# Half-array products of a pair side by side, PSUM in two rotations, and whole products for the last six batches

## The chip, the cores and the metric

The kernel runs on one core of a Trainium2 chip. A core has TensorE (PE, matrix products into PSUM), VectorE (DVE), ScalarE (ACT), GpSimd (POOL) and SyncE (SP, which here issues DMAs). The metric is the device time of one execution in microseconds (us). It was 3108.3 us as the median of three runs (3107.53 to 3109.01).

## The reference

The input x has 128 batches of 128 nodes with 512 features, in fp32; adj is 128x128. Four layers follow each other, each of them `x = layernorm(x + layer(x))`:

```python
# layer 0, W1 = W2 = adj, so that C - A is the bias b alone
A = einsum('od,bdn->bon', W1, x);  C = einsum('od,bdn->bon', W2, x) + b[None, :, None]
out = max(relu(A[:, :, None, :] + (C - A)[:, :, :, None]), axis=-1)
# layer 1: attention with 8 heads of 64 over the 128 nodes
q, k, v = (x @ Wq + bq), (x @ Wk + bk), (x @ Wv + bv)      # each reshaped to (b, n, 8, 64)
scores = einsum('bqhd,bkhd->bhqk', q, k) / sqrt(64) + (1 - adj) * -1e9
out = einsum('bhqk,bkhd->bqhd', softmax(scores), v).reshape(b, n, 512) @ Wo + bo
# layer 2: graph attention
h = x @ W;  e = leaky_relu(h @ a1 [:, :, None] + h @ a2 [:, None, :], 0.2) * adj
out = elu(softmax(e, axis=2) @ h + beta * h)
# layer 3: graph convolution
out = (D^-1/2 adj D^-1/2) @ (x @ weight) + bias
```

## The kernel before

**The planner.** The kernel's work is cut into some 13,000 steps: a name and a batch number, for example ("SC", 60). `STEPS` gives each step its engine, a cost, what it comes after, and the buffers that it takes with the steps that free them. `list_order` is a list scheduler that runs while the kernel is built: it takes the step that can start first by those costs, and among TensorE's steps the one with the lowest `rank`, which is the batch number plus a constant of the step from the table `LAG` minus one from `LEAD`. The instructions are issued in that fixed order. On the chip each engine works through its own queue in order, and waits at an instruction until what it depends on is done. `POOLS` is the number of buffers of each kind; the planner's idea of time has no effect on the chip beyond the order that it leaves.

**The steps of a batch.** Even and odd batches form pairs. LD loads x; A, R and AP0 are layer 0 with its norm. MX1 and MX2 write x to DRAM and read it back turned, TX transposes it in blocks of 32 on VectorE, so that xT is there for the products. RL reads x back for the residual (x2), C1 adds the bias row. The attention: Q, K, V are products with the weights; SC makes the scores of all heads; M adds the mask on VectorE and moves the scores to SBUF; SM1, EXP, SMR, SMN are the softmax (row maximum, exponential, reciprocal, scaling); MS1 and MS2 take the probabilities through DRAM, TS transposes them on VectorE in blocks of 32; O multiplies them with v, and OE copies the result. Y is the product with Wo, then Y1, Q1, P1, AP1 the norm (statistics, `rstd` and `off` on ScalarE, the power -1/2 on POOL, application on ScalarE). Layer 2: L (two dot products), E, EZ, E1, EE, E2 (the softmax), BT and BE (its transpose), GT and GE, U (the product), U1, UE, U2, UP (elu and residual), norm U3 to AP2. Layer 3: NX, NE, C3, Z (the product), norm Z1 to AP3, OUT. The norms' scalars are made once for a pair.

**The products.** `seven` computes a 512x512 product for a pair by seven half-size products instead of eight (P1 to P7), from sums S1 to S4 that POOL makes of the left operand and from weight differences T1 to T4 that are made once; T1 is written over the upper right quarter of the weights, W[0,1]. The seven products run in three PSUM accumulators (px: P1, P2; py: P6, P7, P4; pz: P5, P3), which ScalarE (`u`, `C11`) and VectorE (`U2`, `U3`, `C11`, `C21`, `C22`, `C12`) read out between them; R1 and R2 on POOL add `u` to the residual. Q and K form their result turned, as eight matmuls with 128 columns for a product, the others as four with 256.

**Half-array products.** A score has a contraction over 64 features only, so SC's matmuls use 64 rows of the array each, and two heads (`par` 0 and 1) run in the two halves of the rows. O's results have 64 rows for a head, so its matmuls use 64 columns each. Both are sixteen matmuls for a batch, as the profile counts them: it shows every fp32 matmul of the program as two records, and counts of matmuls in this document are those of the records. In the planner such steps have a `mode`, "row" or "col"; entering or leaving modes costs 0.1 (`SWITCH`), and steps with a mode are drawn together by `CLOSE`. In the order that results, a batch's SC and some other batch's O stand next to each other 107 times, and each of them stands alone 21 times.

**PSUM.** Its eight banks are: one for px, two for py, one for pz, two ("tr") shared by everything else, and two ("sc") for the scores of one batch, one for each `par`.

Lines that matter below: L693 the products of `seven`, L669 its sums on POOL, L752 and L745 its additions on VectorE, L875 the matmuls of SC, L891 M, L906 and L920 the exponential and the scaling, L932 MS2, L940 TS, L950 O, L960 the copies OE, GE, NE, L997 E, L1004 to L1015 EZ and E1, L1035 BT, L1095 NX, L625 the application of a norm.

Of the kernel before, what the change touches and what calls it, by code (L numbers as in the profile page):

```python
# [24 lines left out]
SWITCH = 0.1  # L25
CLOSE = 2.0
REST, WAKE = 1.4, 3.7


class Step:  # L30
# [12 lines left out]
    def __init__(self, engine, cost, *after, takes=(), soon=0.0, batches=None, port=False, mode="",  # L43
                 dma=(), rush=0.0):
        self.port = port or engine == "POOL"
        self.mode, self.dma, self.rush = mode, dma, rush
        self.engine, self.cost, self.after = engine, cost, after
        self.takes, self.soon = dict(takes), soon
        self.batches = batches or (lambda b: True)

    def buffers(self, b):

        return {p: r for p, r in self.takes.items() if b % 2 == 0 or p not in PAIRS}

    def others(self, name, b):
        if name.endswith("+"):
            return [(name[:-1], b), (name[:-1], b ^ 1)]
        if name.endswith("-1"):
            return [(name[:-2], b - 1)]
        if name.endswith("-2"):  # L60
            return [(name[:-2], b - 2)]
        if name.endswith("@"):
            return [(name[:-1], b) for b in (0, 1)]
        return [(name, b)]


def list_order(steps, rank, pools, n):
# [14 lines left out]
    while todo:  # L82
        best = None
        for k in can:
            s = steps[k[0]]
            t = max(ready[k], free.get(s.engine, 0.0), free.get("port", 0.0) if s.port else 0.0)
            for p in s.buffers(k[1]):
                if len(taken[p]) >= pools[p]:
                    for r in taken[p][-pools[p]]:
                        t = max(t, ends.get(r, 1e9) + SIGNAL)  # L90
            if t >= 1e9:
                continue
            if s.engine == "PE":
                key = (t, rank(*k) - (CLOSE if mode and s.mode else 0.0), k)
            else:
                key = (t, ready[k] - s.soon - (s.rush if k[1] < 4 else 0.0), k)
            if best is None or key < best:
                best = key
        t, _, k = best
# [3 lines left out]
        if s.engine == "PE":  # L103
# [4 lines left out]
            if bool(s.mode) != bool(mode):  # L108
                cost += SWITCH
# [8 lines left out]
        for p, readers in s.buffers(k[1]).items():  # L118
# [28 lines left out]
def late(b):  # L147
    return b >= 4


POOLS = {
    "px": 1, "py": 2, "pz": 1, "tr": 2, "sc": 1, "x": 4, "xB": 2, "xT": 2,
    "qT": 2, "kT": 1, "v": 2, "s": 1,
    "sB": 1, "sT": 1, "oT": 1, "x2": 3, "z": 1, "e": 2, "bT": 2, "gT": 1, "m": 1, "x3": 2,
# [7 lines left out]
    "ROW": Step("PE", 3.5, "BV", "BO", takes={"tr": ("ROW1",)}, batches=first),  # L162
    "ROW1": Step("DVE", 0.7, "ROW", batches=first),
    "LOG": Step("DVE", 5.7, "BETA", "A1", batches=first, port=True),
    "LOG1a": Step("PE", 0.45, "LOG", takes={"tr": ("LOG2a",)}, batches=first),
    "LOG1b": Step("PE", 0.45, "LOG", takes={"tr": ("LOG2b",)}, batches=first),
# [3 lines left out]
    "NORM1": Step("PE", 0.2, "NORM", takes={"tr": ("NORM2",)}, batches=first),  # L170
# [3 lines left out]
    "ADJ": Step("PE", 0.2, ("LD", 2.3), takes={"tr": ("ADJ1",)}, batches=first),  # L174
    "ADJ1": Step("DVE", 0.3, "ADJ", batches=first),
    "A": Step("PE", 0.87, "LD", "A-1", "ADJ1@", takes={"tr": ("R",)}),
# [7 lines left out]
    "PT": Step("PE", 0.5, "PX", takes={"tr": ("PTE",)}, batches=early),  # L184
# [5 lines left out]
    "SC": Step("PE", 1.09, mode="row", takes={"sc": ("M",)}),  # L190
    "M": Step("DVE", 1.33, "SC", "MASK@", takes={"s": ("MS1",)}),
# [5 lines left out]
    "MS2": Step("SP", 1.9, "MS1", takes={"sB": ("TS",)}, dma=(4.2, 1.4)),  # L197
    "TS": Step("DVE", 1.18, "MS2", takes={"sT": ("O",)}),
    "O": Step("PE", 1.02, "TS", "VE", "O-1", takes={"tr": ("OE",), "oT": ("Y+",)}, mode="col"),
    "OE": Step("ACT", 0.5, "O"),  # L200
    "Y1": Step("DVE", 0.82, takes={"t1": ("AP1+",)}, soon=20),
    "Q1": Step("ACT", 0.4, "Y1+", soon=20, batches=even),
    "P1": Step("POOL", 0.58, "Q1", soon=20, batches=even),
    "AP1": Step("ACT", 1.03, "P1+", soon=20),
    "L": Step("DVE", 1.45, "AP1", "LOG2a@", "LOG2b@", soon=20, port=True),
    "E": Step("PE", 0.12, "L", takes={"tr": ("E1",)}),
# [4 lines left out]
    "BT": Step("PE", 0.12, "E2", takes={"tr": ("BE",), "bT": ("GT",)}),  # L211
    "BE": Step("ACT", 0.2, "BT", soon=20),
    "GT": Step("PE", 0.89, "BE", "GT-1", takes={"tr": ("GE",), "gT": ("U+",)}),
# [5 lines left out]
    "Q2": Step("ACT", 0.4, "U3+", soon=20, batches=even),  # L219
    "P2": Step("POOL", 0.58, "Q2", soon=20, batches=even),  # L220
    "AP2": Step("ACT", 1.03, "P2+", soon=20),
    "NX": Step("PE", 0.89, "AP2", "NX-1", "NORM2@", takes={"tr": ("NE",), "nx": ("Z+",)}),
# [3 lines left out]
    "Q3": Step("ACT", 0.4, "Z1+", batches=even),  # L226
    "P3": Step("POOL", 0.58, "Q3", batches=even),
    "AP3": Step("ACT", 1.03, "P3+"),
# [16 lines left out]
def sum_steps(n, engine_needs, readers):  # L245

    for i in range(4):
        needs = engine_needs if i == 0 else [f"{n}S{i}"]
        takes = {"SX" if n == "X" else "S": readers} if i == 0 else {}
        STEPS[f"{n}S{i+1}"] = Step("POOL", 0.75, *needs, takes=takes, batches=even, rush=30)  # L250


def seven_steps(n, sums, needs, weights, pool, out, add=(), turned=False, copy=False, T="POOL"):
# [5 lines left out]
    def step(name, engine, cost, *after, takes=(), soon=0.0):  # L259
        after = [(sums if a[0] == "S" else n) + a if isinstance(a, str) else a[0] for a in after]  # L260
        STEPS[n + name] = Step(engine, cost, *after, takes=takes, soon=soon, batches=even)
# [7 lines left out]
    parts += [f"{sums}S{i}" for i in (1, 2, 3, 4)]  # L269
    for s in STEPS.values():  # L270
# [7 lines left out]
        "px": (n + "C11",), "u": (last,), **({"uL": (n + "C21",)} if turned else {}), **out  # L278
    })
    step("P6", "PE", c, "S2", "P1", (n + "T2@",), takes={"py": (n + "C21",)})  # L280
    step("P5", "PE", c, "S1", "P6", takes={"pz": (n + "C12",)})
# [28 lines left out]
for n, needs, letters in (  # L310
# [12 lines left out]
}  # L323
STEPS["SC"].after = ("SC-1", *done["Q"], *done["K"])
STEPS["O"].after = ("TS", "O-1", *done["V"])
STEPS["Y1"].after = tuple(done["Y"])
STEPS["U1"] = Step("ACT", 0.55, *done["U"], takes={"m": ("U2",)}, soon=20)
STEPS["Z1"].after = tuple(done["Z"])
# [3 lines left out]
    "A": 0.325, "QP2": 15.731, "QP7": 15.871, "QP1": 16.057, "QP6": 16.294, "KP6": 16.456,  # L332
    "VP6": 16.608, "QP4": 16.618, "KP1": 17.099, "KP2": 17.121, "KP7": 17.182,
    "KP4": 17.445, "QP5": 17.471, "QP3": 17.625, "KP5": 17.893, "SC": 17.957, "KP3": 18.214,
    "VP1": 18.457, "VP3": 18.722, "VP2": 18.760, "VP4": 18.799, "VP7": 18.889,
    "VP5": 19.214, "O": 21.214, "UP6": 21.481, "YP6": 21.817, "YP1": 22.204, "YP7": 22.289,
    "YP5": 22.388, "YP2": 22.535, "YP3": 22.760, "YP4": 22.812, "UP1": 23.048, "E": 23.322,
    "BT": 23.666, "UP4": 23.847, "GT": 24.012, "UP3": 24.212, "UP7": 24.308, "UP5": 24.501,
    "UP2": 24.787, "NX": 26.260, "ZP3": 26.496, "ZP6": 27.211, "ZP2": 27.845, "ZP1": 27.849,
    "ZP7": 28.155, "ZP4": 28.327, "ZP5": 28.337,  # L340
# [3 lines left out]
    "BT57": 0.32, "O57": 0.32, "Z57": 0.26, "A58": -0.04, "GT58": 0.17, "O58": 0.23, "V58": -0.04,  # L344
    "V59": -1.28, "NX60": 1.25, "Z60": -0.11, "BT61": -0.13, "GT61": 1.45, "O61": 0.43,
    "Y61": -0.05, "Z61": 0.32, "BT62": 0.05, "NX62": 2.93, "U62": -1.85, "Y62": 0.33,
    "BT63": -0.05, "GT63": -0.43, "NX63": 0.07, "O63": 0.21, "U63": 0.77, "V63": -0.28,
}


def rank(name, b):
    if name not in LAG:
        return -1.0
    stage = name[0] if name[1:2] == "P" else name
# [4 lines left out]
def kernel(  # L359
# [39 lines left out]
    def mm_tile(name):  # L399
        return psum.tile([P, 512], F32, tag="tr", name=name, bufs=2)  # L400

    def tr_tile(name):
        return psum.tile([P, C, P], F32, tag="tr", name=name, bufs=2)
# [182 lines left out]
    pa, po, pg, pn, do = {}, {}, {}, {}, {}  # L586
# [12 lines left out]

    def ready(layer, b, shift=None):  # L600

        mv = mean_var.pop((layer, b // 2))
        for held, name in ((rstd, "rstd"), (off, "off")):
            pair_tiny(held, name, layer, b, 1)
        r, o = rstd[layer, b // 2][:, :, 0], off[layer, b // 2][:, :, 0]
# [12 lines left out]
    def power(layer, b):  # L618
        r = rstd[layer, b // 2][:, :, 0]
        nc.gpsimd.tensor_tensor(r, r, neg_half.to_broadcast([P, 2]), ALU.pow)  # L620
# [14 lines left out]
    def seven(n, w, operand, sums, tag, result, added=None, bias=None, scale=1.0):  # L635
# [36 lines left out]
        def P_(name, bank, left, right, new=False):  # L672
            def step(b):
                if new:
                    pool = ("px", "py", "pz")[bank]
                    ps[b, bank] = psum.tile(
                        [P, quarter], F32, tag=pool, name=f"{pool}_{n}{b}", bufs=POOLS[pool]
                    )
# [88 lines left out]
        C_("C12", 2, 0, hi, "own")  # L767
        for i in range(4):
            do[f"{n}T{i}"] = T(i)
# [95 lines left out]
    def SC(b):  # L865
# [3 lines left out]
            psum.tile([P, H // 2, P], F32, tag="sc", name=f"ps_s_{b}_{par}")  # L869
# [17 lines left out]

    def M(b):
        s = probs[b] = buf("s", [P, Q, H, S], b)
        for par, ps in enumerate(scores.pop(b)):  # L890
            nc.vector.tensor_tensor(  # L891
                by_head(s)[:, par * C : (par + 1) * C],
                ps.rearrange("p h (q s) -> p h q s", s=S),
                mask.rearrange("p (q s) -> p q s", s=S)[:, None].to_broadcast([P, C, Q, S]),
                ALU.add,
            )
# [41 lines left out]
    def TS(b):  # L938
        sT[b] = buf("sT", [P, H, P], b)
        nc.vector.transpose(  # L940
            sT[b].rearrange("p h (q s) -> p q h s", s=S), dp.pop(b)
        )

    def O(b):
        ps = tr_tile(f"ps_o_{b}")
        t, vb = sT.pop(b), v.pop(b)[:, b % 2]
        for c in range(C):
            for par in range(2):
# [4 lines left out]
                    rhs=t[:, par * C + c, :],  # L953
# [11 lines left out]
    with_sums("Y", seven("Y", wo_sb, lambda b: oT[b], {}, "x2", x2, x2))  # L965
# [94 lines left out]
    with_sums("U", seven("U", w2_sb, lambda b: gT[b], {}, "x3", x3))  # L1060


    def U1(b):
        m[b] = buf("m", [P, D], b)
        nc.scalar.activation(m[b], x3[b][:, b % 2], AF.Relu, scale=-1.0)
# [4 lines left out]
    def U2(b):  # L1070
        u = x3[b][:, b % 2]
# [119 lines left out]
```

## Time and profile before

| | |
|---|---|
| median of three runs | 3108.3 us |
| the profiled execution, its time | 3107.76 us |
| its span (first to last instruction) | 3106.0 us |
| TensorE busy | 3058.3 us, 98% |
| VectorE / ScalarE / POOL busy | 2346.7 / 2216.0 / 1700.1 us |
| granted TensorE clock, mean | 0.993 |
| SC: matmuls, busy | 2048, 149.2 us |
| O: matmuls, busy | 2048, 140.1 us |

The profiled execution is 1.76 us longer than its span, which is the time around the first and the last instruction. A group's line has, in order: line, engine, operation, output and inputs by the program's names, shapes, count, then busy time and the mean duration of one instruction, and after the second bar the idle time of that engine just before them with what ended it. Matmuls overlap in the records, so durations add up to more than the time they take; the distance between starts is what a step costs TensorE. The granted clock is the share of the full TensorE clock that the throttle allowed in a stretch.

### The profile page before, as it was taken

The numbers are of one execution on the slowest core, as the hardware profiler recorded it, in microseconds if no ns is written. First come the engines' busy times: TensorE is split into PE (matmuls) and PEld (weight loads), VectorE is DVE, ScalarE is ACT, GpSimd is POOL, SyncE is SP. The second block draws the span as 40 slices with busy tenths as digits, with TensorE's granted clock in tenths as the row PEclk, the third lists the DMA queues.
The fourth block names the chain that finished last, engine by engine and source line by source line (L and its number), as shares of the span: only waits on it lengthen the run. The fifth ranks groups of instructions, "written<-read, shape, count | busy, mean of one in ns | idle before, by whom it ended". The sixth has DMA issues, their size and how long they took to land.

```text
span 3106.0 us, 61445 instructions
## 1 busy us (share of the span) xinstructions
PE 3058.3 (98%) x21026; PEld 2709.3 (87%) x21026; DVE 2346.7 (76%) x5418; ACT 2216.0 (71%) x7234; POOL 1700.1 (55%) x1946
## 2 busy tenths in 40 slices
PE   7999999999999999999999999999999999999996
PEld 5888888888888888888888888888888889889875
DVE  6877777777777777777777777777777777777674
ACT  4787777777777777777777777777777777766664
POOL 4345555555655655555555556556555555556475
PEclk8999999999999999999999999999999999999998
DMA  7533332323323323323323233233233232222210
GB/s 211 163 108 102 105 103 96 109 91 108 103 96 102 110 96 103 100 96 105 103 96 109 91 107 103 96 103 109 96 103 100 97 104 89 86 79 89 74 57 28
DMA packets 234457, 312.38 MB, mean 101 GB/s; under 512 B 27680, under 2 KB 156832, under 8 KB 234144
## 3 DMA queue, kind: packets, MB, share of 16 engines
q1 hardware_dynamic: 232368, 307.40, 30.2%
q8 instruction: 166, 2.72, 0.4%
q10 hardware_dynamic: 1776, 1.05, 0.2%
q14 instruction: 147, 1.20, 0.1%
HBM read 174.14 MB, written 134.22 MB: 99 GB/s over the span
## 4 chain that ended last, share of the span: by engine, by line
PE 95%; DVE 1%; DMA 1%; POOL 1%; ACT 1%; issue 1%; ACTq 0%; POOLq 0%; SPq 0%; DVEq 0%
PE py_Q L693 6%; PE py_V L693 6%; PE py_K L693 5%; PE py_U L693 5%; PE py_Y L693 5%; PE py_Z L693 5%; PE ps_s L875 4%; PE ps_o L950 4%; PE px_Y L693 4%; PE px_K L693 4%; PE ps_nx L1095 4%; PE pz_K L693 4%; PE px_Q L693 4%; PE px_U L693 4%; PE ps_gT L1048 4%; PE pz_Q L693 4%
## 5 line engine op out<-in xcount | busy, mean ns | idle before, releaser
L620 POOL TENSOR_TENSOR rstd<-rstd,neg_half 128x2 f32<-128x2 f32 x256 | 176.8, 698 | 508.6 <-ACT rstd L606 505.4
L625 ACT ACTIVATE x<-x,off,rstd 128x512 f32<-128x512 f32 x512 | 417.0, 814 | 17.1
L906 ACT ACTIVATE s<-s,mx 128x128 f32<-128x128 f32 x1024 | 395.6, 391 | 18.9 <-DVE mx L900 15.1
L597 DVE BATCH_NORM_STATS2 st<-x 128x6 f32<-128x512 f32 x512 | 346.7, 677 | 10.3 <-POOL x L1076 5.5
L920 ACT ACTIVATE s<-s,sm 128x128 f32<-128x128 f32 x1024 | 313.5, 393 | 6.5 <-DVE sm L915 5.7
L1076 POOL TENSOR_TENSOR x<-x,x 128x512 f32<-128x512 f32 x128 | 162.8, 1272 | 183.1 <-DVE x L1072 174.7
L984 DVE SCALAR_TENSOR_TENSOR junk<-x,wa_bc 128x512 bf16<-128x512 f32 x256 | 230.0, 898 | 16.4 <-ACT x L625 5.5
L669 POOL TENSOR_TENSOR S_U<-gT 128x256 f32<-128x256 f32 x128 | 117.2, 915 | 189.9 <-ACT gT L960 189.7
L606 ACT ACTIVATE rstd<-mv,eps_c 128x2 f32<-128x2 f32 x256 | 75.6, 295 | 200.6 <-DVE mv L598 194.0
L826 POOL TENSOR_TENSOR x<-x,bo_bc 128x512 f32<-128x512 f32 x128 | 160.7, 1277 | 98.2 <-DMA x<-dx 88.2
L1109 POOL TENSOR_TENSOR x<-x,b_bc 128x512 f32<-128x512 f32 x128 | 162.8, 1272 | 64.5 <-PE ps_nx L1095 57.7
L906 ACT ACTIVATION_READ_ACCUMULATOR s<-s,mx 128x1 f32 x1024 | 194.7, 190 | 0.0
L940 DVE STREAM_TRANSPOSE sT<-sB 128x1024 f32<-128x1024 f32 x128 | 158.8, 1240 | 35.7 <-PE ps_o L950 35.5
L891 DVE TENSOR_TENSOR s<-ps_s,mask 128x512 f32<-128x512 f32 x256 | 162.2, 674 | 10.1 <-PE ps_s L875 5.7
L624 ACT ACTIVATE off<-off,rstd 128x1 f32<-128x1 f32 x512 | 147.2, 288 | 21.5 <-POOL rstd L620 21.4
L1040 ACT COPY bT<-ps_bT 128x128 f32<-128x128 f32 x128 | 33.9, 265 | 175.9 <-PE ps_bT L1035 175.6
L1095 PEld LDWEIGHTS ps_nx<-naT,x 128*128 128x128 f32 x1024 | 131.6, 195 | 29.3 <-issue 23.0
L900 DVE TENSOR_REDUCE mx<-s 128x8 f32<-128x1024 f32 x128 | 153.9, 1203 | 0.2
L875 PEld LDWEIGHTS ps_s<-kT,qT 64*128 64x128 f32 x2048 | 124.5, 187 | 33.4 <-issue 30.7
L875 PE MATMUL ps_s<-kT,qT 64*128 64x128 f32 x2048 | 149.2, 285 | 0.4 <-DVE s L891 0.3
L752 DVE TENSOR_TENSOR x<-py_Z,x 128x256 f32<-128x256 f32 x192 | 80.4, 419 | 90.0 <-PE py_Z L693 87.1
L669 POOL TENSOR_TENSOR S_Y<-oT 128x256 f32<-128x256 f32 x128 | 93.5, 731 | 95.1 <-ACT oT L960 73.5
(180 smaller groups left out, 9312.7 us busy)
## 6 DMA issues: line engine op xcount, KB each, us to landing
dp<-s SPq DMA_DIRECT2D x128, 512.0 KB, 2.6
sB<-dp SPq DMA_DIRECT2D x512, 128.0 KB, 2.8
x<-in_x SPq DMA_DIRECT2D x128, 256.0 KB, 3.2
dx<-x SPq DMA_DIRECT2D x128, 256.0 KB, 4.4
x<-dx SPq DMA_DIRECT2D x64, 512.0 KB, 4.0
out_x<-x SPq DMA_DIRECT2D x128, 256.0 KB, 2.0
xB<-dx SPq DMA_DIRECT2D x496, 64.0 KB, 2.0
wk_sb<-in_L_gnn_Wk SPq DMA_DIRECT2D x4, 256.0 KB, 8.3
```

What stands on the lines that cost most here:

```text
L597: nc.vector.bn_stats(st, t)
L620: nc.gpsimd.tensor_tensor(r, r, neg_half.to_broadcast([P, 2]), ALU.pow)
L625: nc.scalar.activation(dst, src, AF.Identity, bias=shift, scale=scale)
L669: nc.gpsimd.tensor_tensor(s[:, i], x, y, op)
L693: nc.tensor.matmul(to, lhsT=one, rhs=two, start=(new and k == 0), stop=(k == 1), skip_group_check=True,)
L875: nc.tensor.matmul(scores[b][par][:, c, :], lhsT=qT[b][rows, c, cols], rhs=kT[b][rows, c, cols], start=True, stop=True,)
L906: nc.scalar.activation(s[:, :, h], s[:, :, h], AF.Exp, bias=mx[:, h : h + 1], accum_out=sums[b][:, h : h + 1],)
L920: nc.scalar.activation(s[:, :, h], s[:, :, h], AF.Identity, scale=sm[:, h : h + 1])
L984: nc.vector.scalar_tensor_tensor(junk, x2[b][:, b % 2], 1.0, wa_bc[i], op0=ALU.mult, op1=ALU.mult, accum_out=s12[b][:, i : i + 1],)
L1076: nc.gpsimd.tensor_tensor(t, t, x2.pop(b)[:, b % 2], ALU.add)
L1095: nc.tensor.matmul(ps[:, c, :], lhsT=x3[b][:, b % 2, c * P : (c + 1) * P], rhs=naT, start=True, stop=True,)
L1109: nc.gpsimd.tensor_tensor(t, t, b3_bc, ALU.add)
```

## The change

It has four parts.

1. *Order.* The planner's costs of entering a mode are set apart (`ENTER`: row, col and back to whole-array products), steps of the same mode are drawn together more strongly, a mode step may be chosen up to 0.15 ahead of its being ready (`AWAIT`), and SC and O of both batches of a pair get the same batch number in `rank`. `LAG` and `LEAD` have new values throughout. In the order that results there are 59 groups of SC, O, O, SC in direct succession (the scores of one pair and the outputs of an earlier pair), 3 of SC and O, 2 of O and O, 7 lone SC and 3 lone O.
2. *PSUM.* The banks px, py, pz and tr become one rotation of five (`ps`), and the scores a rotation of three (`sc`). M becomes M0 and M, one for each half of the heads, so that the first bank is free after M0.
3. *Transposed probabilities.* TS writes over its input: `sB` has two buffers, `sT` is gone. O's moving operand is then four runs of 32 elements instead of one run of 128, and `sB` is freed by O instead of by TS.
4. *The last six batches* (from `LAST` = 122 on) form Y, U and Z as whole products, batch by batch: F0 and F1 of 8 matmuls each, into one bank, added to the residual by YFE and ZFE (U's product is read by U1 and U2 directly). The overwritten quarter of the weights is read again from DRAM by YR, UR and ZR on SP's queue, after the last seven of that product. The norms Q1 to Q3 and P1 to P3 run for single batches there.

```diff
-SWITCH = 0.1
+ENTER = {"row": 0.2, "col": 0.15, "": 0.205}
 CLOSE = 2.0
+AWAIT = 0.15
...
-            if s.engine == "PE":
-                key = (t, rank(*k) - (CLOSE if mode and s.mode else 0.0), k)
+            if s.engine != "PE":
+                key = (t, ready[k] - s.soon - (s.rush if k[1] < 4 else 0.0), k, t)
+            elif mode and s.mode:
+                near = CLOSE + (CLOSE if s.mode == mode else 0.0)
+                key = (max(t - AWAIT, free["PE"]), rank(*k) - near, k, t)
             else:
-                key = (t, ready[k] - s.soon - (s.rush if k[1] < 4 else 0.0), k)
+                key = (t, rank(*k), k, t)
...
 POOLS = {
-    "px": 1, "py": 2, "pz": 1, "tr": 2, "sc": 1, "x": 4, "xB": 2, "xT": 2,
+    "ps": 5, "sc": 3, "x": 4, "xB": 2, "xT": 2,
     "qT": 2, "kT": 1, "v": 2, "s": 1,
-    "sB": 1, "sT": 1, "oT": 1, "x2": 3, "z": 1, "e": 2, "bT": 2, "gT": 1, "m": 1, "x3": 2,
+    "sB": 2, "oT": 1, "x2": 3, "z": 1, "e": 2, "bT": 2, "gT": 1, "m": 1, "x3": 2,
...
-    "SC": Step("PE", 1.09, mode="row", takes={"sc": ("M",)}),
-    "M": Step("DVE", 1.33, "SC", "MASK@", takes={"s": ("MS1",)}),
+    "SC": Step("PE", 0.895, mode="row", takes={"sc": ("M0",), "sc+": ("M",)}),
+    "M0": Step("DVE", 0.665, "SC", "MASK@", takes={"s": ("MS1",)}, soon=3),
+    "M": Step("DVE", 0.665, "M0", soon=3),
...
-    "MS2": Step("SP", 1.9, "MS1", takes={"sB": ("TS",)}, dma=(4.2, 1.4)),
-    "TS": Step("DVE", 1.18, "MS2", takes={"sT": ("O",)}),
-    "O": Step("PE", 1.02, "TS", "VE", "O-1", takes={"tr": ("OE",), "oT": ("Y+",)}, mode="col"),
+    "MS2": Step("SP", 1.9, "MS1", takes={"sB": ("O",)}, dma=(4.2, 1.4)),
+    "TS": Step("DVE", 1.18, "MS2"),
+    "O": Step("PE", 0.875, "TS", "VE", "O-1", takes={"ps": ("OE",), "oT": ("Y+",)}, mode="col"),
...
-    "Q1": Step("ACT", 0.4, "Y1+", soon=20, batches=even),
+    "Q1": Step("ACT", 0.4, "Y1", "Y1*", soon=20, batches=normed),
...
+    STEPS[n + "R"] = Step("SP", 0.4, n + "P5-2", dma=(2.5, 0.9), batches=lambda b: b == LAST)
+    STEPS[n + "F0"] = Step("PE", 1.74, need, n + "R%", n + "F0-1", takes={"ps": (end,), **out}, batches=last)
+    STEPS[n + "F1"] = Step("PE", 1.74, n + "F0", batches=last)
+STEPS["YFE"] = Step("DVE", 0.69, "YF1", "C1", soon=20, batches=last)
+STEPS["ZFE"] = Step("DVE", 0.69, "ZF1", "C3", soon=20, batches=last)
...
+    if name in ("SC", "O") and b in BOTH:
+        b |= 1
     return b + LAG[name] - LEAD.get(f"{stage}{b // 2}", 0.0)
...
+        def again(b):
+            nc.sync.dma_start(
+                out=T1, in_=source[:quarter, hi].rearrange("(c p) f -> p c f", p=P)
+            )
+        def whole(half):
+            def step(b):
+                if half == 0:
+                    ps[b] = mm_tile(f"p_{n}{b}")
+                cols = (lo, hi)[half]
+                for k in range(C):
+                    nc.tensor.matmul(
+                        ps[b][:, cols],
+                        lhsT=operand(b)[:, b % 2, k],
+                        rhs=w[:, k, cols],
+                        start=(half == 0 and k == 0),
+                        stop=(k == C - 1),
+                        skip_group_check=True,
+                    )
+                if half == 1:
+                    full[b] = ps.pop(b)
+            return step
...
     def TS(b):
-        sT[b] = buf("sT", [P, H, P], b)
-        nc.vector.transpose(
-            sT[b].rearrange("p h (q s) -> p q h s", s=S), dp.pop(b)
-        )
+        sT[b] = dp.pop(b)
+        nc.vector.transpose(sT[b], sT[b])
...
-                    rhs=t[:, par * C + c, :],
+                    rhs=t[:, :, par * C + c, :],
...
+    def add_full(held):
+        def step(b):
+            t = held[b][:, b % 2]
+            nc.vector.tensor_tensor(t, full.pop(b), t, ALU.add)
+        return step
```

## The prediction

> **What bounds the kernel now.** I read the page first: the span, the busy shares, the chain that ended last.
>
> ```profile
> span 3106.0 us, 61445 instructions
> PE 3058.3 (98%) x21026; PEld 2709.3 (87%) x21026; DVE 2346.7 (76%) x5418; ACT 2216.0 (71%) x7234; POOL 1700.1 (55%) x1946
> PE 95%; DVE 1%; DMA 1%; POOL 1%; ACT 1%; issue 1%; ACTq 0%; POOLq 0%; SPq 0%; DVEq 0%
> ```
>
> TensorE carries 95% of the chain, so the change is priced in TensorE time. Then busy time by stretches, to see where TensorE is not dense:
>
> ```profile
> 1000.00:2000.00 1000.00, 1000.00 (x6948) 892.07 (x6947) 767.11 (x1777) 733.23 (x2386) 551.55 (x632) 1.00 0.31 101
> ...
> 3000.00:3050.00 50.00, 41.63 (x220) 33.30 (x220) 36.38 (x85) 27.39 (x73) 34.58 (x39) 0.97 0.09 32
> 3050.00:3106.00 56.00, 36.62 (x151) 29.15 (x149) 19.91 (x45) 21.77 (x50) 26.79 (x29) 0.80 0.08 28
> ```
>
> The columns are the stretch, its length, busy time and count of PE, PEld, DVE, ACT and POOL, the granted TensorE clock, and DMA. The middle has no TensorE idle time; the last 106 us have 28 us of it, and a clock of 0.97 and then 0.80. Last, TensorE's instructions in order of time, in the dense part:
>
> ```profile
> 1502.39 1.03 PE L693 MATMUL py_Z<-ZT,S_Z 128*128 128x256 f32 x4
> 1503.26 1.05 PE L693 MATMUL pz_K<-SX_V,wk_sb 128*128 128x128 f32 x8
> 1504.24 1.09 PE L950 MATMUL ps_o<-sT,v 128*64 128x128 f32 x16
> 1505.27 1.16 PE L875 MATMUL ps_s<-kT,qT 64*128 64x128 f32 x16
> 1506.36 1.16 PE L693 MATMUL py_Q<-SX_V,QT 128*128 128x128 f32 x8
> 1507.36 0.27 PE L997 MATMUL ps_e<-ident,s 128*128 128x128 f32 x1
> ```
>
> Durations overlap, so starts are what counts: py_Z takes 0.87. The pz_K ahead of O takes 0.98 and the py_Q behind S takes 1.00, where others of that form take 0.89: entering half-array products costs 0.09, leaving 0.10. Between them O takes 1.02 and S 1.09, and the same numbers stand alone or in the other sequence (a batch's O and S are adjacent 107 times, apart 21 times each). The starts of single records inside a group say why: after the first pair, O starts a pair of matmuls every 0.109 (eight pairs: 0.87), S every 0.112 (0.90); the first pair takes 0.05 (O) or 0.10 (S) more, and the last is followed by 0.10 (O) or 0.09 (S).
>
> **The change part by part.**
>
> *Scores and outputs side by side.* By its instruction order the new program has 59 quartets S O O S, 3 lone S-O, 7 lone S, 3 lone O, 2 O O. Before: a side-by-side S and O costs 0.09+1.02+1.09+0.10 = 2.31, a lone S 1.29, a lone O 1.22; 107x2.313+21x1.289+21x1.221 = 300.2 us. After: in a quartet the first O has no exit (0.92) and the second no entrance (0.97): 0.09+1.09+0.92+0.97+1.09+0.10 = 4.28 against 4.63; with the rest 59x4.278+3x2.313+7x1.289+3x1.221+2x2.094 = 276.2. Difference **-24.0**. No O follows an O in this trace: the joint lies between a pair's ordinary pitch (nothing extra, since inside O the column halves alternate in the same way) and a full exit and entrance (0.15, 61 joints, +9). I take nothing.
>
> *O reads the transposed probabilities as four runs of 32 elements*, since VectorE now transposes in place. No matmul of this trace has such an operand. The nearest row is ScalarE's exponential, with and without those runs:
>
> ```profile
> L906 ACT ACTIVATE s<-s,mx 128x128 f32<-128x128 f32 x1024 | 395.6, 391 | 18.9 <-DVE mx L900 15.1
> L1021 ACT ACTIVATE e<-e,nmx 128x128 f32<-128x128 f32 x128 | 50.9, 397 | 34.3 <-DVE nmx L1015 34.3
> ```
>
> L906 reads one head of the same layout (4 runs of 32), L1021 a contiguous tile: 391 against 397 ns. I take 0. Lower end -1.5% of O (-2 us); upper end: no overlap at all, a pair taking its whole recorded 273 ns for 109, 1.31x128 = +168. The Trainium skill, "Advanced Engine Details and Errata", section Memory Cachelines, speaks on both sides: an SBUF read keeps full speed while following accesses stay in a 16-byte line (a run of 32 fp32 does), but under PSUM it says "Any non-contiguous AP significantly slows down matmuls". By the first the sum stays at 3063; if the second held for an SBUF operand too, half rate as an estimate would make it 3175. No matmul of this trace settles it. The in-place transpose is the same 1.24 us, off the path.
>
> *Three score banks, mask in two steps.* The second S of a quartet needs the bank that M0, the mask add of the first S, frees. VectorE runs M0 behind E1 of an earlier batch, whose transpose E stands on TensorE directly ahead of the quartet. In the trace E's start to the end of E1 is 1.88 at least, 2.13 median, 2.76 at the ninetieth percentile. E starts 0.20 before S, so M0 (0.68) is done 1.93+0.68+0.06 = 2.67 after S starts at the median; S is due again at 1.09+0.92+0.97 = 2.99. Cover 0.32: cost 0; at 2.76 it is 0.31x60 = +19. Behind M0 on VectorE wait M, the row maximum and U2, whose readers stand many products later.
>
> *Five banks in rotation for six fixed ones.* Steps that had a bank of their own may now wait for another's evacuation. The nearest row is the first px product of Y and U, 0.08 slower than its second (0.95 and 0.86 at 1510.12). If Q, K, V and Z got that too: 4x64x0.08 = +20; if Y and U lost it: -10. I take 0, as the middle shows no wait.
>
> *SP.* The probabilities' reload MS2 now waits for O of two batches (sB lives until then) instead of a transpose, with RL, OUT and the next loads queued behind. SP already waits 458 us on that release, without TensorE waiting: loads run well ahead. 0; the transpose has a whole 48 us pair period. Three 256 KB reloads (W's upper right quarter, overwritten at the start) join SP's queue near the end. A 256 KB load lands in 3.2 us (L427; 8.3 for wk_sb in the crowded start). Y's has over 40 us, U's about 11, Z's 4.7 of TensorE work (half a seven, two NX, two small) ahead of its reader. 0; at 8.3, +3.6.
>
> *Whole products.* For three pairs in each of Y, U, Z a seven of 7x4 matmuls (6.06) becomes 2x16 (6.92 at 0.216 a matmul): 9x0.87 = **+7.8**. Removed with it: the sums S1 to S4 on POOL (0.74 to 0.92 each) and the interleaved evacuations.
>
> *The tail.* From 3000.07 TensorE issues 58 products of four (0.866), 12 of eight (0.893), 8 transposes (0.11), 2 O (0.875): 63.5 us, in 97.1 until 3097.2. With 0.7 for switches, **32.9 are lost**. The waits say to what:
>
> ```profile
> PE py_Z L693 <- POOL S_Z L669: 5.0, 2, 2.6
> PE ps_nx L1095 <- ACT x L625: 3.8, 2, 2.7
> ...
> PE py_U L693 <- POOL S_U L669: 2.6, 1, 2.6
> PE py_U L693 <- DVE x L752: 2.0, 2, 1.3
> ```
>
> These are the sums and corrections inside the last sevens, and norms waiting for both batches of a pair; the rest is half clock. The whole products need no sums and the last norms run batch by batch. What is late next? From U's product to NX: 0.52+0.53+0.72+1.27+0.87+0.3+0.7+1.1 = 6.0 and signals. Behind U126 the new order has U127, NX124, NX125, Z124, Z125: 12.2 of TensorE work; behind U125, 9.6. From E to BT about 3.3 against 4.4. Everything is covered once, by 1 to 6 us, so clock and idle loss should nearly go. I keep 5 of it (between 0 and all 33; nearest to the covers just counted): **-28**.
>
> *The end.* From the last product to the span's end 8.85. One 128x512 add (0.69, L550) instead of a 0.42 one, and one application instead of two (1.0): **-0.7**. The start (24 us lost in the first 200) has the same loads and nearly the same order: 0, +-4.
>
> Sum: 3106.0-24.0+7.8-28-0.7 = 3061.1 of span. The profiled execution took 3107.76, 1.76 beyond its span: 3062.9. The median of the runs is 0.5 higher: **3063**.
>
> **The rivals.**
> *A wait in each quartet or bank rotation eats the gain from the switches.* For it: a cover of only 0.32, met 60 times. Against: the same chain of E, ScalarE and E1 meets its median in half of the cases. At the ninetieth percentile 3063+19 = 3082; with bank waits on top to 3100.
> *The tail stays as it is*: whole products cost 7.8, and the loss only changes its place: 3063+28 = 3091. For it: last stages are one dependent chain. Against: the covers counted above.
> *O slows down through its strided operand.* It ends above 3108: the gain is 45 us over 128 O, so it decides from 0.35 us per O (a pair every 153 ns instead of 109). At double pitch 128x0.87 = +112: 3175. Against it: the two exponentials; for it: no matmul row.
> *The change does not do what it says*: excluded for the order, which shows the quartets; possible for the joint O to O alone (+9, inside the range).
>
> **How the numbers follow.** Forecast case (3052 to 3075) 0.70, the quartet or bank wait 0.15, tail unchanged 0.05, slow O 0.10. Low end: nothing of the tail's 5 stays (-5), start 4 better, O 2 better: 3052. High end: the forecast with the ninetieth-percentile wait and a reload at 8.3: 3063+19+4 = 3086; what is above is a bit of the second case, the third and the fourth, about 0.2. Faster by over 0.2% (about what this kernel's runs can tell) 0.89, within 0.02, slower 0.09 (slow O).
>
> **What would show it.** Right: ps_o as 128 O in groups of two, O to O 0.92, S to O 1.09; no wait of ps_s on VectorE; middle still without idle TensorE, one pair in about 0.35 us less; the clock at 1.00 until the last 15 us; 28 products of the new line at 1.73 each behind the last O. Wrong: O's pitch above 109 ns, ps_s or a px product in the list of waits with more than 10 us, or a clock below 1 near 3030.

## The result and the profile after

The changed kernel takes 3056.35 us as the median of four runs (3053.99 to 3057.54), the kernel before 3108.11 as the median of four (3107.53 to 3109.01). The ratio is 0.9832, 95% interval 0.9815 to 0.9849: 1.7% faster. The forecast was 3063, between 3052 and 3086. The profiled execution took 3057.54, with a span of 3055.6.

The page of the changed kernel, first the busy shares and the chain that ended last:

```profile
span 3055.6 us, 61911 instructions
PE 3021.9 (99%) x21062; PEld 2706.8 (89%) x21062; DVE 2350.8 (77%) x5379; ACT 2215.0 (72%) x7240; POOL 1624.7 (53%) x1907
PE 94%; DVE 3%; DMA 2%; ACT 1%; issue 0%; SPq 0%; POOL 0%; ACTq 0%; POOLq 0%; DVEq 0%
```

TensorE still carries the chain, with 36 us less of busy time, and its idle time went from 48 to 34 us. Busy time by stretches (the stretch, its length, then PE, PEld, DVE, ACT and POOL, the granted clock, DMA):

```profile
1000.00:2000.00 1000.00, 998.74 (x7013) 899.16 (x7013) 781.20 (x1796) 741.59 (x2419) 541.43 (x640) 1.00 0.32 102
...
2950.00:3000.00 50.00, 50.00 (x312) 43.98 (x311) 35.42 (x87) 34.08 (x96) 23.74 (x28) 1.00 0.19 59
3000.00:3055.60 55.60, 47.18 (x248) 41.37 (x246) 23.96 (x56) 29.22 (x76) 21.30 (x25) 0.98 0.12 43
```

In the middle 7013 matmuls fit into a thousand microseconds where 6948 did: most of that is the edges, the rest is in the table below. In the last 55.6 us TensorE is idle for 8.4, of which 7.2 lie behind the last matmul and 1.1 are a single wait of a py_Z; the last 106 us of before had 28, and a clock of 0.97 and 0.80. TensorE in order of time shows a quartet, that is S O O S in direct succession:

```profile
1541.54 0.27 PE L1117 MATMUL ps_bT<-ident,e 128*128 128x128 f32 x1
1541.65 0.27 PE L1079 MATMUL ps_e<-ident,s 128*128 128x128 f32 x1
1541.85 1.16 PE L945 MATMUL ps_s<-kT,qT 64*128 64x128 f32 x16
1542.95 1.97 PE L1024 MATMUL ps_o<-sB,v 128*64 128x128 f32 x32
1544.84 1.16 PE L945 MATMUL ps_s<-kT,qT 64*128 64x128 f32 x16
1545.93 1.13 PE L737 MATMUL px_Z<-w_sb,nx 128*128 128x256 f32 x4
1546.90 1.03 PE L737 MATMUL py_Z<-ZT,S_Z 128*128 128x256 f32 x4
```

By the starts: first S 1.09, both O together 1.89 (0.92 and 0.97 in the single records, medians over the 59 quartets 0.924 and 0.973), second S 1.09, the product behind it 0.97. That is the sum of the prediction, 4.28 with the entrance, to the hundredth.

To see where the 50.4 us of span went, I took for each execution the starts of all TensorE steps. From the distance of two starts I took off the pitch of that step, which is its time in dense stretches (0.865 for four matmuls, 0.892 for eight 128 wide, 1.73 for half a whole product, 0.109 for a transpose), and the edges, which is what entering and leaving half-array products costs. What is left over is time that TensorE lost:

| | before | after | difference | predicted |
|---|---|---|---|---|
| edges of S and O | 300.2 | 276.2 | -24.0 | -24.0 |
| whole products for sevens | | | +7.8 | +7.8 |
| lost in the first 200 us | 24.3 | 29.7 | +5.3 | 0 +-4 |
| lost from 200 to 2900 us | 12.0 | 5.4 | -6.6 | 0 |
| lost from 2900 us to the last product | 34.1 | 2.8 | -31.3 | -28 |
| behind the last product | 8.8 | 7.4 | -1.4 | -0.7 |

They sum to -50.2; the remaining 0.2 is rounding. The lines of the edges and of the whole products are counts of steps times their measured times; the other lines are what is left of the distances of starts. A second profiled execution of the changed kernel (span 3054.5) lost 28.1 in the first 200 us and within 0.5 the same elsewhere.

### The profile page after: what moved, and what is told of

Read it like the earlier page. It is cut to its first block, busy times and chain, and to the rows that moved or that the text cites. A ratio compares the mean times of both kernels' runs of the same rounds, so it can differ in the third digit from the quotient of the medians.

```text
span 3055.6 us, 61911 instructions
## 1 busy us (share of the span) xinstructions
PE 3021.9 (99%) x21062; PEld 2706.8 (89%) x21062; DVE 2350.8 (77%) x5379; ACT 2215.0 (72%) x7240; POOL 1624.7 (53%) x1907
## 4 chain that ended last, share of the span: by engine, by line
PE 94%; DVE 3%; DMA 2%; ACT 1%; issue 0%; SPq 0%; POOL 0%; ACTq 0%; POOLq 0%; DVEq 0%
PE py_Q L737 6%; PE py_K L737 5%; PE py_U L737 5%; PE py_Y L737 5%; PE py_V L737 5%; PE py_Z L737 5%; PE ps_s L945 4%; PE pz_Q L737 4%; PE px_K L737 4%; PE pz_K L737 4%; PE ps_o L1024 4%; PE ps_nx L1181 4%; PE px_Q L737 4%; PE ps_gT L1130 4%; PE px_Z L737 4%; PE pz_V L737 4%
## 5 line engine op out<-in xcount | busy, mean ns | idle before, releaser
L667 POOL TENSOR_TENSOR rstd<-rstd,neg_half 128x2 f32<-128x2 f32 (+1 forms) x265 | 182.3, 688 | 149.9 <-ACT rstd L653 149.7
L716 POOL TENSOR_TENSOR SX_V<-xT 128x256 f32<-128x256 f32 x128 | 93.7, 732 | 272.2 <-PE py_Y L737 243.8
L1034 ACT COPY nx<-ps_nx 128x512 f32<-128x512 f32 x128 | 74.9, 585 | 215.9 <-PE ps_nx L1181 215.6
L1066 DVE SCALAR_TENSOR_TENSOR junk<-x,wa_bc 128x512 bf16<-128x512 f32 x256 | 207.1, 809 | 14.8 <-ACT x L672 4.0
L796 DVE TENSOR_TENSOR x<-py_U,u_U 128x256 f32<-128x256 f32 x183 | 77.6, 424 | 151.8 <-PE py_U L737 151.3
L959 DVE TENSOR_TENSOR s<-ps_s,mask 128x512 f32<-128x512 f32 x256 | 169.1, 682 | 9.3 <-DMA dp<-s 5.8
L716 POOL TENSOR_TENSOR S_U<-gT 128x256 f32<-128x256 f32 x122 | 93.0, 762 | 128.8 <-ACT gT L1034 128.6
L1016 DVE STREAM_TRANSPOSE sB<-sB 128x1024 f32<-128x1024 f32 x128 | 157.9, 1234 | 0.8 <-DMA sB<-dp 0.8
L737 PEld LDWEIGHTS px_K<-xT,wk_sb 128*128 128x128 f32 x1024 | 133.8, 192 | 27.3 <-issue 23.6
L854 PE MATMUL ps_a<-x,adjT 128*128 128x512 f32 x256 | 134.4, 609 | 6.5 <-DMA x<-in_x 6.5
```

What stands on the lines that cost most here:

```text
L667: nc.gpsimd.tensor_tensor(r, r, neg_half.to_broadcast([P, r.shape[1]]), ALU.pow)
L716: nc.gpsimd.tensor_tensor(s[:, i], x, y, op)
L737: nc.tensor.matmul(to, lhsT=one, rhs=two, start=(new and k == 0), stop=(k == 1), skip_group_check=True,)
L959: nc.vector.tensor_tensor(by_head(probs[b])[:, par * C : (par + 1) * C], scores[b][par].rearrange("p h (q s) -> p h q s", s=S), mask.rearr ...
L1066: nc.vector.scalar_tensor_tensor(junk, x2[b][:, b % 2], 1.0, wa_bc[i], op0=ALU.mult, op1=ALU.mult, accum_out=s12[b][:, i : i + 1],)
```

## The experiments

All times are medians, taken beside the kernel before on the same chip (which took 3108.6, 3107.6 and 3108.3 beside the three groups of kernels). The changed kernel, run once more beside the second group, is the base for differences.

> The changed kernel beside the others of this call, for its own spread on this chip: 3054 to 3058.

Measured: 3056.26 (3054.49 to 3057.29).

### Are the edges what the order pays?

One ordinary product goes between the two O of each quartet:

```diff
-        for _, name, b in list_order(STEPS, rank, POOLS, B):
+        for _, name, b in apart(list_order(STEPS, rank, POOLS, B)):
             do[name](b)
# apart: in TensorE's S O O S ZP1, ZP1 goes ahead of the second O
```

> The changed kernel (3056 us) with one ordinary product, the first px of Z that stood behind the quartet, moved between its two O: S O X O S. Nothing else moves. Theory (the gain of the order is edges): one exit and one entrance more for each of 59 quartets, 0.15 at the two O and 0.10+0.09 at the ordinary product: 59 x 0.348 = +20.5, so 3077, and the trace shows O alone at 1.02 with 0.96 for the px_Z. Rival (the gain comes from the banks, or the second S was held back anyway and the product only fills its wait): within 3 us of 3056.

Measured: 3088.36, +32.1. Its TensorE in order of time:

```profile
1555.99 1.09 PE L1042 MATMUL ps_o<-sB,v 128*64 128x128 f32 x16
1557.01 1.13 PE L755 MATMUL px_Z<-w_sb,nx 128*128 128x256 f32 x4
1558.08 1.09 PE L1042 MATMUL ps_o<-sB,v 128*64 128x128 f32 x16
1559.10 1.16 PE L963 MATMUL ps_s<-kT,qT 64*128 64x128 f32 x16
1560.19 1.13 PE L755 MATMUL py_Z<-ZT,S_Z 128*128 128x256 f32 x4
1561.31 1.13 PE L755 MATMUL px_Z<-w_sb,nx 128*128 128x256 f32 x4
1562.27 1.05 PE L1148 MATMUL ps_gT<-bT,x 128*128 128x128 f32 x8
```

O takes 1.02 twice and px_Z between them 1.06 (0.10 behind one edge and 0.09 ahead of the next), so the edges cost the 0.348 expected, 20.5 us in 59 quartets. The other 11.6 are not edges: py_Z behind the quartet takes 1.12 where a product behind an S takes 0.97, and the second px_Z 0.97 where 0.86 is its pitch. 0.25 in 59 quartets is 14.9; some 3 us of small waits of the changed kernel, most of them at pz_Y, went away. The list of the weight loads' waits names the place:

```profile
PEld px_Z L755 <- ACT u_Z L775: 22.8, 59, 0.4
```

I moved one step, and the second px_Z came 0.86 nearer to the quartet. It needs u_Z, which ScalarE makes of the first px_Z. That product now comes earlier, but u_Z kept its place in ScalarE's queue, and ends only 0.05 ahead of the second px_Z; py_Z's 1.12 is the same wait, seen from the product ahead.

With two products moved in, S X O Y O S:

```diff
# as above, and ZP1 ahead of the first O, ZP6 ahead of the second
```

> The changed kernel with two ordinary products moved into each quartet: S X O Y O S. Theory: against the quartet 59 x (0.348 + 0.197) = +32.2, so 3089; the step from one product to two is another 59 x 0.197 = 11.6. Rival (only the joint of the two O matters, S beside O is worth nothing): as the one-product version, 3077. Second rival (the edges cost nothing): 3056.

Measured: 3150.15, +93.9, far above the forecast. The list of TensorE's waits has a new first line, and the order of time the place:

```profile
PE px_Z L756 <- ACT u_Z L776: 61.6, 59, 1.0
```

```profile
1588.60 1.16 PE L964 MATMUL ps_s<-kT,qT 64*128 64x128 f32 x16
1590.81 1.13 PE L756 MATMUL px_Z<-w_sb,nx 128*128 128x256 f32 x4 [1.04 <-ACT u_Z L776]
```

The second px_Z now stands right behind the quartet and needs u_Z, which ScalarE makes of the first px_Z; ScalarE's queue has it at its old place. 61.6 for this wait and 32.2 for the edges make 93.8. That this meets the 93.9 so closely is partly chance: by the distance of starts the wait is 1.11, 65.7 in 59 quartets, and some 4 us of the changed kernel's small losses are gone. So the theory's forecast of the time failed in both versions, by 11 and 61 us of waits that it did not have, and it holds in both for what it priced (O 1.02 and the products between 1.06 in each). Both rivals fall: neither are the edges free, nor does the joint of the two O alone count. The total of a move is edges plus what the move brings too early.

### Does the second S hang on the first mask step?

```diff
# mask_late: where VectorE's order is M0 M U2, U2 goes first
```

> The changed kernel with VectorE's U2 (0.7 us) moved ahead of M0 and M in the 59 quartets, so that the first score bank comes free later. In the changed kernel's trace M0 starts 1.66 after the first S and ends 0.6 before the second S is due; U2's input is there 1.98 after the first S, so M0 would end about 3.4 and the second S wait about 0.47. Theory (the third score bank carries the quartet, its cover is about 0.6 us): 59 x 0.47 = +28, between +20 and +32, so 3076 to 3088, and the list of waits gets a line of ps_s on VectorE's mask add. Rival (the second S does not hang on M0): 3056 within 2 us.

Measured: 3085.48, +29.2 (3084.01 to 3087.78). TensorE in order of time:

```profile
1553.00 1.16 PE L962 MATMUL ps_s<-kT,qT 64*128 64x128 f32 x16
1554.09 1.97 PE L1041 MATMUL ps_o<-sB,v 128*64 128x128 f32 x32
1555.98 1.70 PE L962 MATMUL ps_s<-kT,qT 64*128 64x128 f32 x16
1557.61 1.13 PE L754 MATMUL px_Z<-w_sb,nx 128*128 128x256 f32 x4
```

The second S takes 1.64 from start to start instead of 1.09: 0.544 in 59 quartets is 32.1, less some 3 us of small waits that are gone. So a VectorE instruction of 0.7 us in the wrong place costs more than all the edges save. One thing of the forecast was wrong: the list of TensorE's waits has no line of ps_s. Asked for the scores' tile, the same trace puts the wait elsewhere:

```profile
who waited for it (us, times):
  PEld ps_s L962: 15.2, 59
```

It stands at the weight load (PEld), and with half its size; the distance of the starts had all of it.

### What closed the tail?

```diff
-LAST = 122
+LAST = 128     # whole_none;  126 in whole_pair
```

> The changed kernel with sevens to the end (no whole products, no single norms; the order of the middle is the same). Theory: TensorE gets 7.8 us of work less, and the 31 us of idle time and half clock that the change took out of the tail come back, a little more or less since this tail's order was not made for it: +23, between +17 and +33, so 3073 to 3089, and the last 50 us show a clock below 0.9. Rival (the tail is dense because of the new order and the PSUM rotation, not because of the whole products): -7.8, 3049.

> The changed kernel with whole products for the last pair alone (two batches instead of six). Theory (each pair treated so takes its share of the tail's loss away, the last one most): 5.2 us of work less than with six, and between a third and two thirds of the 31 us back: 3056 - 5 + 10 to 20, so 3061 to 3071. Rival (the last pair alone matters, since the chain ends with it): 3051.

Measured: 3093.15 without whole products (+36.9), 3083.30 with the last pair alone (+27.0). The end of whole_none by stretches:

```profile
2950.00:3000.00 50.00, 42.27 (x248) 35.23 (x247) 34.36 (x81) 28.86 (x82) 31.64 (x36) 0.93 0.16 53
3000.00:3050.00 50.00, 34.60 (x167) 29.13 (x166) 27.26 (x67) 23.62 (x60) 28.80 (x32) 0.85 0.06 22
3050.00:3092.40 42.40, 26.60 (x109) 21.27 (x107) 13.87 (x31) 13.51 (x30) 19.41 (x21) 0.82 0.07 25
```

From 2900 on it loses 47.5 us against 2.8; less the 7.8 of work that it saves that is the +36.9. Its first wait:

```profile
PE ps_nx L1181 <- ACT x L672: 14.3, 4, 8.7
```

NX waits for the application of a norm, which needs both batches of the pair. whole_pair loses 38.2, and gives back 5.2 of work; that would be +30, and its profiled execution was 2.8 above its median. So the rival (this order and rotation keep the tail dense by themselves) is refuted, and so is the idea that the last pair alone counts. Both came out above their ranges (3073 to 3089 and 3061 to 3071): a tail of sevens loses more here than in the kernel before, which lost 34.1. I put that down to `LAG` and `LEAD`, which were chosen with whole products; this is not shown. What whole products are worth is 34.1-2.8-7.8 = 23.5 us against the tail of before, and 37 against sevens in the new order. Both figures hold for whole products together with the norms of single batches, since `LAST` switches both; neither was run alone, and no order made for sevens with the new banks was tried.

### The 6.6 us in the middle

Before, the first px product of Y took 0.95 and that of U 0.95, in nearly every pair, where 0.86 is the pitch, and a py of U 0.90. In the changed kernel all three take 0.86; with 51, 54 and 53 pairs in the stretch they are 11.5 us, and 4.9 us of small new waits (pz_Y, pz_V and others) stand against it. In the record of before, ScalarE's read-out of px for Q ends at 1510.05, and px_Y starts at 1510.12, with a first matmul that takes 472 ns where 379 is the rule:

```profile
1509.42 0.63 ACT L706 ACTIVATE qT<-px_Q,bq_sb 128x128 f32<-128x128 f32 x2 [0.58 <-PE px_Q L693]
```

```profile
1510.12 1.12 PE L693 MATMUL px_Y<-wo_sb,oT 128*128 128x256 f32 x4
1511.07 1.03 PE L693 MATMUL pz_Z<-w_sb,S_Z 128*128 128x256 f32 x4
```

To see if that is the bank, the kernel before with px_Y a step later:

```diff
# px_later, on the kernel before: YP1 behind the ZP5 that followed it, UP1 behind UP6
```

> The kernel before (3108 us) with one swap in TensorE's order: the first px product of Y goes behind the pz product that followed it (49 pairs), the first px product of U behind the py product of U that followed it. Theory (before, these two met a px bank whose read-out by ScalarE had only just ended, and paid 0.09 each; the rotation of five took that away and this is the 6.6 us that the middle gained beyond the edges): both take 0.86 again, -4.4 and -4.5, so 3099. Rival (the 0.09 belongs to the operand, oT or gT, or to the product itself): 3108 within 1 us, and the 0.95 stays with px.

Measured: 3132.45, +24.9, against both theory and rival. The trace has px_Y at 0.86, but in U the swap moved the first py ahead of the sum that it reads: NX ahead of it takes 0.26 more, and pz_V ahead of the second py 0.31 more, with 0.07 for each of the two py. These 0.71 in 51 pairs are 36. The half that could be read, Y, was run alone:

```diff
# px_y_later: only YP1 behind ZP5
```

> The kernel before (3108) with one swap: the first px product of Y goes behind the pz product of Z that followed it, in 49 pairs; the swap in U is left out. Theory (px_Y came 0.07 after ScalarE's read-out of its only bank had ended and paid 0.09): px_Y takes 0.86 and the time falls by 49 x 0.09 = 4.4, to 3103 or 3104. Rival (the swap's other effects eat it): 3107 to 3109 with px_Y at 0.86.

Measured: 3104.12, ratio to the kernel before 0.9986 (0.9977 to 0.9995), -4.1. The trace of that version:

```profile
1508.08 1.03 PE L710 MATMUL pz_Z<-w_sb,S_Z 128*128 128x256 f32 x4
1508.94 1.03 PE L710 MATMUL px_Y<-wo_sb,oT 128*128 128x256 f32 x4
1509.81 1.03 PE L710 MATMUL py_Y<-YT,S_Y 128*128 128x256 f32 x4
```

The same product with the same operands takes 0.87 when it comes one step later, so the 0.09 does not belong to the product or its operand. For the bank speaks the whole trace of before: of the 230 px products of Y and U between 200 and 2900 us, 105 start less than 0.1 us behind the end of their bank's read-out, and all of them take 0.93 to 0.97. Of the other 125, whose bank was free at least 0.36 us earlier, all take 0.86 to 0.87 but three that stand beside half-array products. The operands of the 105 were complete 1.7 us or more before. What in TensorE takes the 0.09 is not shown, and U was not tried alone.

### O's operand in runs

The trace after has already settled the price of four runs of 32: none (O's single records are 0.109 a pair in both kernels). Three versions go on from there, on the changed kernel. Each makes O multiply other elements of the transposed probabilities, so their attention is not the reference's; the work has the same size.

```diff
-                    rhs=t[:, :, par * C + c, :],
+                    rhs=t.rearrange("p q h s -> p (q h s)")[:, (par * C + c) :: 8],        # o_step
+                    rhs=...[:, :, 4 * j : 4 * j + 4]   # o_runs4: 32 groups of 32, four of each
+                    rhs=...[:, :, 2 * j : 2 * j + 2]   # o_runs2: 64 groups of 16, two of each
```

> The changed kernel with O's moving operand read at a step of eight elements (128 single elements, 32 bytes apart) instead of four runs of 32. O multiplies other elements of the transposed probabilities, so this version's attention is not the reference's. Theory (TensorE reads fp32 at any step at full rate): O stays at 0.92 and 0.97, 3056. Rival (what counts is that following elements share a 16-byte line, as the Trainium skill's page Advanced Engine Details and Errata, section Memory Cachelines, says of SBUF: four runs of 32 do, this does not): slower; at half rate, as an estimate, 128 x 0.87 = +112, 3168.

> The changed kernel with O's moving operand read in 32 runs of four elements (16 bytes each) instead of four runs of 32. O multiplies other elements of the transposed probabilities, so this version's attention is not the reference's. Theory A (what counts is how many elements are read of one 16-byte line): O at 0.92 and 0.97, 3056. Theory B (every new run costs something): between that and the single-element version's 3178, nearer to it by the number of runs: a quarter of the 122 us, 3087.

> The changed kernel with O's moving operand read in 64 runs of two elements (8 bytes each). O multiplies other elements of the transposed probabilities, so this version's attention is not the reference's. Theory A (two elements of a line suffice, as the Trainium skill's page Advanced Engine Details and Errata says in the section Memory Cachelines): O at 0.92 and 0.97, 3056. Theory B (every new run costs something): half of the 122 us, 3117. Theory C (a line must be read whole): as with single elements, 3178.

Measured: 3177.88 with single elements (+121.6), 3054.37 with runs of four, 3055.38 with runs of two. TensorE with single elements, then with runs of two:

```profile
1552.00 3.93 PE L1024 MATMUL ps_o<-sB,v 128*64 128x128 f32 x32
1555.85 1.16 PE L945 MATMUL ps_s<-kT,qT 64*128 64x128 f32 x16
```

```profile
1540.73 1.98 PE L1024 MATMUL ps_o<-sB,v 128*64 128x128 f32 x32
1542.64 1.16 PE L945 MATMUL ps_s<-kT,qT 64*128 64x128 f32 x16
```

Two O take 3.85 from start to start against 1.91 (1.90 with long runs); in the single records a pair starts every 0.232 instead of every 0.109. Runs of two cost 0.01 an O. So it is not the number of runs (theory B), but whether an element comes alone. Single elements nearer than 32 bytes were not tried, so these runs do not tell an element that is alone in its 16 bytes from the step of 32 bytes itself. The Trainium skill, "Advanced Engine Details and Errata", section Memory Cachelines, says that two hits on a 16-byte line suffice and that a new line for each access costs; the runs agree with it, with these numbers.

### The start

The changed kernel's trace has 2.3 us of waiting that end at 89.5 us, behind VectorE's one-time block LOG, and then a granted clock of 0.63 up to 93.1. (In its second profiled execution the same wait is there, 2.33, and the clock stays at 1.00; that is most of the 1.6 us between the two in the first 200.) The block went behind the two read-outs that follow it:

```diff
# log_later: LOG behind VU3 of pair 2, LOG1a behind VP4 of pair 2
```

> The changed kernel (3056) with VectorE's one-time block LOG (8 sums over weight rows, 6.96 us) placed behind the two read-outs of Q and V that stood behind it, and its TensorE step LOG1a placed behind the two products that these release. In the changed kernel TensorE waits 2.3 us there and then runs some 3.4 us at half clock. Theory (the start lost what it did to this block): -2.3 and up to -1.7, so 3052 to 3054. Rival (the block only moves the wait to the next read-out, QU3, which is now the one behind it): 3056 within 1 us.

Measured: 3058.68 (3057.72 to 3060.06), 2.4 above the changed kernel, which was not run beside it; the kernel before was 0.7 higher there too. Neither the theory's 3052 to 3054 nor the rival's 3056 was met. Its list of waits:

```profile
PE py_Q L749 <- DVE qT L801: 4.9, 1, 4.9
```

The wait went to the next read-out of Q, which now stands behind the block, and doubled: the rival is right in its mechanism. No version that computes the reference's function came out faster than the changed kernel.

## Why the prediction was right, point by point

*Edges, -24.0.* Right in mechanism and size: the numbers of a lone S, a lone O and their neighbours in the trace before hold for the quartet, and no exit or entrance is paid at O to O. The two versions that take quartets apart show the price again, under waits of their own.

*The strided operand, 0.* Right. The row it rested on, ScalarE's exponential with and without the runs, gave the right answer; it is a row of another engine, so that it carried over to TensorE was a guess that held, and only the trace after shows it (0.109 a pair). The single-element version shows that a price as large as the rival's (3178 measured, 3175 at double pitch) was there to be paid with another layout.

*Three score banks, 0.* Right: by the scores' tile only VectorE itself waits on the mask (0.6 us), never TensorE, and the second S takes 1.09 in all 59 quartets. My cover of 0.32 was too small: it took the median of E to E1 over orders that the new program does not have. In the changed kernel M0 starts 1.66 behind the first S, so that the cover is about 0.6; delaying M0 by an instruction of 0.7 cost 29 us.

*Five banks, 0.* Mis-sized, as was the sum's other 0 for the middle. Measured: -6.6 there. I had named -10 as the lower end, for px_Y and px_U losing their 0.08, and chose 0. The rows before had the cause in them: two products 0.09 slow in nearly every pair, each right behind the read-out of its only bank. Small new waits of 4.9 us stand against them.

*Whole products and tail, +7.8 and -28.* Right in mechanism; the loss that stays is 2.8 instead of 5. The covers counted from the order (12.2 or 9.6 us of work against a chain of 6) were enough. Taking the whole products out, and the norms of single batches with them, brings the loss back.

*The end, -0.7*: mis-sized, measured -1.4. The sum left out the statistics of the pair's second batch, which stood behind the last addition before (0.66) and do not after. *The start, 0 +-4*: mis-sized, measured +5.3 in the profiled execution (+3.7 in the second). The lists of waits have 3.0 more at ps_x, which waits for VectorE, and 2.3 at the py_Q behind LOG; why the order came out so there is open.

*SP and its reloads, 0.* Right: no product of line L824 waits in the trace.

The median came out 6.7 below the point, inside the range: -6.6 from the middle, -3.3 from the tail and -0.7 from the end, against +5.3 in the start, make -5.3 of the 5.5 that the span lies below the 3061.1 of the sum. The median of the runs lies 1.2 below the profiled execution, where the sum added 0.5. That the misses in the middle and in the start nearly cancel is luck. The rivals: no wait took the gain back, the tail closed, and O kept its pitch.

## What to carry to other kernels

Where one engine is dense, price an order by the distance of starts: the edges between kinds of matmuls, read off a few neighbouring lines, gave the 24 us. A move on that engine has a second price, since what follows it comes earlier and may meet the read-outs of other engines that kept their places; take it from a new trace and not from the edge, and look at the waits of the weight loads too. At the end of a program with long chains, 14% more matmuls in a simpler form, without sums between, can pay when the chain leaves the engine idle and its clock lowered (0.80 in the last 56 us of before, 0.50 from 3090 to 3093): here 7.8 us of work against 31 us of loss.

## What the runs showed of the hardware that was not expected

A matmul that came 0.07 us after the read-out of its bank had ended still took 0.09 longer, and no list of waits shows it; in the version with the late mask step a wait of 0.54 in each quartet appears in the lists only at half its size, at the weight load. A wait of 2.3 us near the start was followed by a clock of 0.63 over 3.6 us in one execution and by 1.00 in another of the same program. TensorE reads an fp32 moving operand at full rate in runs of two elements (8 bytes), and at 0.47 of it (0.109 for 0.232 a pair) when each element stands alone, 32 bytes from the next.
